# A conditioned transformer block on one core: first norms through four columns, and the last output products by a seven-product scheme

## The chip, the cores and the metric

The kernel runs on one core of one Trainium2 chip. The metric is the device time of one launch in microseconds (us). Before the change the median of three runs is 2432.27 us, with 2431.27 the lowest and 2441.08 the highest.

## What is computed

`x` is 4 x 1024 x 512 and `t` (the condition) 4 x 128, all in float32. One block with 16 heads of 32 and a hidden width of 2048 is applied, and its input is added once more at the end:

```
norm(x, t, gw, gb, bw, bb):
    g, b = t @ gw.T + gb, t @ bw.T + bb
    return g * x * rsqrt(mean(x*x) + 1e-6) + b
attention(x): q, k, v = x @ Wq.T, x @ Wk.T, x @ Wv.T
    softmax(q k.T / sqrt(32)) v, then @ Wo.T
x1  = x  + attention(norm(x, t, g1..., b1...))
x2  = x1 + (silu(h @ gate_w.T) * (h @ hid_w.T)) @ out_w.T,  h = norm(x1, t, g2..., b2...)
out = x + x2
```

## The kernel before, in words

Features lie on the 128 partitions and tokens along the free axis. The tokens are cut into 8 blocks of 512 (`NBLK`), two for each of the 4 batch items; the 512 features are 4 chunks of 128 (`C`).

**Start (L707 to L738).** The first two blocks are loaded, and `norm_sum` (L210) makes the inverse root of the first: ScalarE (ACT) squares each chunk (L215), TensorE (PE) sums it over the partitions by a product with a constant matrix `ones_mean` (L216), which leaves the mean in all 128 partitions; ACT takes the root (L218), VectorE (DVE) the reciprocal (L219), each over 128x512. `modulation` (L718) makes the gains and shifts from `t` with 8 small products. `norm_rest` scales on DVE (L199) and modulates on ACT (L202). Then keys and queries are projected (`project_kq`), the second block is normed in the same way, and values are projected (`project_v`).

**Main loop (L774, step g).** Each g computes scores for one `raw` tile (4 heads x 256 keys x 256 queries, from 10 buffers), copies them out of PSUM, takes maxima, subtracts, exponentiates, and multiplies by the values. The row sums of the softmax come from adding the exponentials of four tiles: the first tile is the accumulator, and the other three are added to it by DMAs on GpSimd's queue (L396), one after another. DVE folds the result (L404), PE sums it over partitions (`sums`, L414). There are 256 raw tiles.

From g = 60 (`FS`) on the feed-forward part of earlier blocks is worked in between, one hidden tile p of 128 in two g. Gate and hidden products are made by Winograd's form of Strassen's scheme: seven half-width products (2 matmul passes of 256 columns each) in place of eight, in the methods `pair_15` to `pair_4`; DVE and ACT make the sums between them in PSUM. The output projection is plain: four hidden tiles form a group, and each p runs one `contract` (L576) of four passes of 512 columns over the group before, for one of the 4 output chunks d. `take_contract` (L580) adds half the product to the residual `res` and, with the last group of a block, sends `out`.

**Tail (L935 to L976).** When attention is done (g = 268, p0 = 104), p runs on alone to 127, and four more `contract` calls finish group 31. `mm` (L109) splits each 128x128 weight into four 32-column parts here, which run beside each other.

**Order.** On PE, DVE, ACT and GpSimd the order is the one the program writes. SP's queue, which issues nearly all loads and stores, is ordered by the framework's scheduler, which places a DMA where it expects its buffer to be free; SP then waits in that order. The scores have four banks of PSUM (`ps_sc`), other products two (`ps`, tag `w`), one (`ps_av`) and one (`ps_b`).

Of the kernel before, what the change touches and what calls it, by code (L numbers as in the profile page):

```python
# [10 lines left out]
F32 = mybir.dt.float32  # L11
BF16 = mybir.dt.bfloat16
AF = mybir.ActivationFunctionType
ALU = mybir.AluOpType
# [3 lines left out]
P = 128  # L18
NB = 512
# [5 lines left out]
def tile_cond_transformer_block(  # L25
# [33 lines left out]
    ps_sc = ctx.enter_context(tc.tile_pool(name="ps_sc", bufs=1, space=PSUM))  # L59
    ps_av = ctx.enter_context(tc.tile_pool(name="ps_av", bufs=1, space=PSUM))  # L60
    ps = ctx.enter_context(tc.tile_pool(name="ps", bufs=2, space=PSUM))
    ps_b = ctx.enter_context(tc.tile_pool(name="ps_b", bufs=1, space=PSUM))


    ident = const.tile([P, P], F32, tag="ident", name="ident")
# [143 lines left out]

    def norm_sum(dst, tag: str):  # L210

        pm = ps.tile([P, NB], F32, tag="w", name=f"pm{tag}")
        for c in range(C):
            sq = sb.tile([P, NB], F32, tag="h", name=f"sq{tag}_{c}", bufs=7)
            nc.scalar.activation(sq, dst[:, c, :], AF.Square)  # L215
            nc.tensor.matmul(pm, ones_mean, sq, start=(c == 0), stop=(c == C - 1))  # L216
        inv = sb.tile([P, NB], F32, tag="rmax" if tag == "a0_0" else "tot", name=f"inv{tag}", bufs=1)
        nc.scalar.activation(inv, pm, AF.Sqrt, bias=eps)  # L218
        nc.vector.reciprocal(inv, inv)  # L219
# [312 lines left out]
    def pair_26(p: int):  # L532
        a = bank_a[p]
        product(a[:, LEFT], fw[p, 0][:, 1], tokens(p // NF)[2])
        product(a[:, RIGHT], fw[p, 1][:, 1], state["sums"][:, 1])
# [49 lines left out]
            nc.sync.dma_start(out=out[n][:, d, :], in_=r)  # L585


    NR = NBLK * C * (NB // HQ) * UN
    GB = C * (NB // HQ)
    BS = GB * UN  # L590
# [113 lines left out]
    with tc.manual_schedule(  # L704
# [29 lines left out]
        for kt in range(KT // 2):  # L734
            project_v(0, kt)()
            if kt == 0:
                modulation(1)
        project_kq(0, 0, 0, 1)()  # L738

# [2 lines left out]
        g = 0  # L742
        END = NR + 12
        NP_ = NBLK * NF

        def filler(p: int, tail: bool = False):
# [9 lines left out]
            if q + 1 < NP_:  # L756
# [178 lines left out]
        p0 = (END - FS) // 2  # L935
        for p in range(p0, NP_):
# [24 lines left out]
            evict()  # L961
            if p == p0:
                pm = ps.tile([P, NB], F32, tag="w", name=f"pmf{n}")
                for c in range(C):
                    nc.tensor.matmul(pm, ones_mean, squares[c], start=(c == 0), stop=(c == C - 1))
                inv = sb.tile([P, NB], F32, tag="tot", name=f"invf{n}", bufs=1)
                nc.scalar.activation(inv, pm, AF.Sqrt, bias=eps)
                nc.vector.reciprocal(inv, inv)
                state[f"f{n}"] = inv
            if p == p0 + 1:  # L970
                norm_rest(1, n // QB, x2[n], f"f{n}")
        for p in range(NP_, NP_ + FG):
            one, two, evict = filler(p)
            one()
            two()
            evict()  # L976


# [39 lines left out]
```

## Time and profile before

| what | value |
|---|---|
| median of three runs | 2432.27 us |
| profiled execution, its own time | 2435.25 us |
| its span (first to last instruction) | 2433.4 us |
| mean granted clock of TensorE | 0.998 |
| PE busy | 2378.9 us, 98% |
| DVE busy | 1938.6 us, 80% |
| ACT busy | 1412.7 us, 58% |
| accumulating DMAs (L396) | 192, 1024 KB each, 9.2 us to landing (median) |

A row of the page's groups or of the order of time gives an engine, a line of the kernel, what is written and read, and durations. PE and PEld are matmuls and the loads of their weights; a float32 product shows as two rows of each. The idle time in brackets is that of the engine before the instruction, with what released it. Ends of matmuls are modelled, and their rows overlap; the distance between starts is what counts. DMA rows on a queue (SPq, POOLq) show the issue; the time to landing stands in the table of DMA issues.

### The profile page before, as it was taken

What the parts mean: (1) busy time and instruction counts of PE and PEld (TensorE: products, weight loads), DVE (VectorE), ACT (ScalarE), POOL (GpSimd) and SP (SyncE); (2) the same over time, 40 slices, a digit from 0 to 9 for tenths busy, and PEclk for the clock granted to TensorE, in tenths of its full rate; (3) what the DMA queues carried; (4) which work ended last, traced back from release to release, by engine and by line L of the source; (5) the groups of instructions that cost most, each with busy time, mean ns of one, the idle gap of its engine ahead of it and who ended that gap; (6) DMA issues with size and microseconds to landing.
All of it is one profiled execution on the core that took longest, in us unless ns stands there. A gap on an engine that the chain in (4) does not pass through costs nothing. (4 is left out here: it accounts for less than half of the span.)

```text
span 2433.4 us, 72676 instructions
## 1 busy us (share of the span) xinstructions
PE 2378.9 (98%) x32553; PEld 1131.6 (47%) x32553; DVE 1938.6 (80%) x2183; ACT 1412.7 (58%) x1495; POOL 172.4 (7%) x207
## 2 busy tenths in 40 slices
PE   8999999999999999999999999999999999999999
PEld 3333334345454544545454545454545454434444
DVE  2688988888799988998899979997999799833322
ACT  3677777766566656755576657665666576512110
POOL 0000000000000000000000000000000000000000
PEclk9999999999999999999999999999999999999999
DMA  6599999988889788989888888898888889853442
GB/s 216 167 302 262 263 247 248 224 223 228 199 203 218 193 229 204 215 210 231 196 210 217 223 200 211 208 232 211 200 206 214 218 202 216 198 143 118 144 129 71
DMA packets 185988, 501.79 MB, mean 206 GB/s; under 512 B 21319, under 2 KB 78663, under 8 KB 158286
## 3 DMA queue, kind: packets, MB, share of 16 engines
q0 software_dynamic: 28656, 208.68, 44.3%
q1 hardware_dynamic: 156734, 288.47, 35.4%
q8 instruction: 256, 4.19, 0.7%
q14 instruction: 54, 0.44, 0.1%
q10 hardware_dynamic: 288, 0.01, 0.0%
HBM read 246.44 MB, written 41.97 MB: 119 GB/s over the span
## 5 line engine op out<-in xcount | busy, mean ns | idle before, releaser
L369 DVE TENSOR_TENSOR raw<-raw,shift 128x2048 f32<-128x2048 f32 (+1 forms) x320 | 588.8, 1856 | 26.1 <-ACT shift L364 26.1
L323 ACT COPY raw<-sc 128x2048 f32<-128x2048 f32 x256 | 479.6, 1873 | 181.6 <-PE sc L316 123.0
L372 ACT ACTIVATE raw<-raw 128x2048 f32<-128x2048 f32 x256 | 491.0, 1918 | 149.8 <-DVE raw L369 147.3
L328 DVE TENSOR_TENSOR rmax<-rmax,raw 128x1024 f32<-128x1024 f32 x384 | 469.5, 1223 | 47.5 <-ACT raw L323 41.2
L112 PE MATMUL pc<-h,ow 128*32 128x512 f32 x4096 | 469.1, 595 | 3.0 <-DMA ow<-in_out_w 2.1
L396 POOL DMA_DIRECT2D raw<-raw x192 | 165.3, 861 | 1944.9 <-ACT raw L372 864.3
L316 PE MATMUL sc<-q,k 32*128 32x256 f32 x4096 | 293.3, 400 | 1.1 <-ACT raw L323 1.1
L382 PE MATMUL av<-raw,v 128*32 128x256 f32 x4096 | 271.9, 383 | 21.6 <-ACT raw L372 21.1
L112 PE MATMUL pa<-x,fa 128*32 128x256 f32 x4096 | 269.9, 381 | 3.7 <-DVE pa L530 2.7
L112 PE MATMUL pa<-sums,fw 128*32 128x256 f32 x4096 | 267.9, 379 | 0.0
L112 PEld LDWEIGHTS pc<-h,ow 128*32 128x32 f32 x4096 | 128.3, 110 | 247.7 <-issue 226.6
L316 PEld LDWEIGHTS sc<-q,k 32*128 32x128 f32 x4096 | 184.9, 184 | 117.5 <-issue 74.9
L112 PE MATMUL pkq<-y,wkq 128*32 128x512 f32 (+1 forms) x1664 | 231.4, 594 | 4.3 <-ACT y L202 4.1
L112 PEld LDWEIGHTS pa<-x,fa 128*32 128x32 f32 x4096 | 123.4, 109 | 120.7 <-DVE pa L530 21.1
L112 PEld LDWEIGHTS pa<-sums,fw 128*32 128x32 f32 x4096 | 133.0, 110 | 88.0
L382 PEld LDWEIGHTS av<-raw,v 128*32 128x32 f32 x4096 | 110.4, 109 | 134.9 <-ACT raw L372 50.8
L583 DVE SCALAR_TENSOR_TENSOR res<-pc,res 128x512 f32<-128x512 f32 x128 | 88.2, 689 | 73.3 <-PE pc L112 70.4
L562 ACT ACTIVATE t<-pa 128x512 f32<-128x512 f32 x128 | 78.3, 611 | 109.9 <-PE pa L112 109.6
L545 ACT COPY pb<-pa 128x256 f32<-128x256 f32 x128 | 46.2, 361 | 164.3 <-PE pa L112 163.0
L112 PE MATMUL pb<-x,fw 128*32 128x256 f32 x2048 | 134.0, 379 | 1.2 <-ACT pb L545 1.2
L112 PE MATMUL pa<-x,fw 128*32 128x256 f32 x2048 | 134.0, 379 | 0.0
L112 PE MATMUL pb<-sums,fa 128*32 128x256 f32 x2048 | 133.9, 379 | 0.0
(108 smaller groups left out, 2163.9 us busy)
## 6 DMA issues: line engine op xcount, KB each, us to landing
raw<-raw POOLq DMA_DIRECT2D x192, 1024.0 KB, 9.2
fw<-sw SPq DMA_DIRECT2D x128, 512.0 KB, 7.1
fa<-in_gh_w SPq DMA_DIRECT2D x128, 384.0 KB, 6.1
ow<-in_out_w SPq DMA_DIRECT2D x128, 256.0 KB, 3.2
wkq<-in_kq_w SPq DMA_DIRECT2D x32, 512.0 KB, 6.3
v<-vs SPq DMA_DIRECT2D x128, 128.0 KB, 6.0
k<-kqs SPq DMA_DIRECT2D x124, 128.0 KB, 7.3
kqs<-st SPq DMA_DIRECT2D x61, 256.0 KB, 9.2
```

What stands on the lines that cost most here:

```text
L112: nc.tensor.matmul(dst[k : k + n, :], w[:, k : k + n], moving, start=start, stop=stop, skip_group_check=seeded)
L316: nc.tensor.matmul(sc[:, i, k, :], keys[rows, k * P : (k + 1) * P], queries[rows, :], start=True, stop=True)
L323: nc.scalar.copy(raw[r].rearrange("p k h q -> p h k q"), state.pop(("sc", r)))
L328: nc.vector.tensor_tensor(rmax[j], rmax[j], raw[r][:, k, :, :], ALU.max)
L369: nc.vector.tensor_tensor(t, t, s.unsqueeze(1).to_broadcast(list(t.shape)), ALU.add)
L372: nc.scalar.activation(raw[r], raw[r], AF.Exp)
L382: nc.tensor.matmul(av[j][i * DH : (i + 1) * DH, :], v[m, u][:, k, i * DH : (i + 1) * DH], raw[r][:, k, i, :], start=(kt == 0), stop=(kt == ...
L396: nc.gpsimd.dma_start(out=acc[j].rearrange("p k h q -> p (k h q)"), in_=raw[r].rearrange("p k h q -> p (k h q)"), accum_op=ALU.add,)
L545: nc.scalar.copy(bank_b[p][:, RIGHT], bank_a[p][:, RIGHT])
L562: nc.scalar.activation(state["t", p], bank_a[p], AF.Tanh, scale=0.5)
L583: nc.vector.scalar_tensor_tensor(r, pp, 0.5, r, ALU.mult, ALU.add)
```

## The change

It has four parts.

1. `norm_sum` for the first two blocks. The squares of the four chunks are added on DVE, and four products with a single column of `ones_mean` bring the means of the 512 tokens into 128 partitions x 4 columns. Root and reciprocal work on these four columns. DVE multiplies an identity matrix by them (`diagonal`), and one product of `ones_mean` with the diagonal spreads the inverse to all partitions, into PSUM (`spread_root`), from where the scaling reads it. The two tiles of the inverse in SBUF go.
2. `warm` multiplies constants: five products ahead of the first norm, one before and one after its spread. The second norm's spread comes after the first value projection.
3. From p = 108 (`seven`) on, and for the last group, the output projection uses the scheme of seven products over pairs of output chunks and pairs of hidden tiles (`output_steps`). Four banks are taken from the scores' pool, which is closed at p0, and two of them are seeded with a constant product. The weights of all four groups are loaded once into `raw` buffers, 16 loads of 256 KB (`output_sums`), and their sums are made on DVE at p = 106 to 109 (`output_sums_add`); the sums of the hidden halves are made on DVE at the end of each group (`hidden_sums`). Loads of `ow` stop at q = 103.
4. The last group runs both pairs of chunks in turn, step by step, in place of four `contract` calls.

```diff
-        pm = ps.tile([P, NB], F32, tag="w", name=f"pm{tag}")
+        sq = [sb.tile([P, NB], F32, tag="h", name=f"sq{tag}_{c}", bufs=7) for c in range(C)]
         for c in range(C):
-            sq = sb.tile([P, NB], F32, tag="h", name=f"sq{tag}_{c}", bufs=7)
-            nc.scalar.activation(sq, dst[:, c, :], AF.Square)
-            nc.tensor.matmul(pm, ones_mean, sq, start=(c == 0), stop=(c == C - 1))
-        inv = sb.tile([P, NB], F32, tag="rmax" if tag == "a0_0" else "tot", name=f"inv{tag}", bufs=1)
-        nc.scalar.activation(inv, pm, AF.Sqrt, bias=eps)
-        nc.vector.reciprocal(inv, inv)
-        state[tag] = inv
+            nc.scalar.activation(sq[c], dst[:, c, :], AF.Square)
+            if c:
+                nc.vector.tensor_tensor(sq[0], sq[0], sq[c], ALU.add)
+        nt = NB // P
+        pm = ps.tile([P, nt], F32, tag="w", name=f"pm{tag}")
+        for t in range(nt):
+            nc.tensor.matmul(pm[:, t : t + 1], sq[0][:, t * P : (t + 1) * P], ones_mean[:, 0:1], start=True, stop=True)
+        few = sb.tile([P, nt], F32, tag="few", name=f"few{tag}", bufs=2)
+        nc.scalar.activation(few, pm, AF.Sqrt, bias=eps)
+        nc.vector.reciprocal(few, few)
+        diagonal = sb.tile([P, nt, P], F32, tag="t", name=f"diagonal{tag}", bufs=2)
+        nc.vector.scalar_tensor_tensor(
+            diagonal, ident..., float(D), few..., ALU.mult, ALU.mult)
+
+        def spread_root():
+            inv = ps.tile([P, NB], F32, tag="w", name=f"inv{tag}")
+            nc.tensor.matmul(inv, ones_mean, diagonal.rearrange("p t q -> p (t q)"), start=True, stop=True)
+            state[tag] = inv
+        return spread_root
...
+    def output_sums(f: int, k: int):
+        w = sb.tile([P, 16, P], F32, tag="raw", name=f"wt{f}_{k}", bufs=RAW)
+        for i in range(2):
+            nc.sync.dma_start(out=w[:, 4 * i : 4 * i + 4, :], in_=out_w[f, 2 * k + i])
+        state["wt", f, k] = w
+
+    def output_sums_add(f: int, k: int):
+        w = state["wt", f, k]
+        a11, a12, a21, a22, s1, s2, s3, s4 = (w[:, i : i + 2, :] for i in range(0, 16, 2))
+        nc.vector.tensor_tensor(s1, a21, a22, ALU.add)
+        nc.vector.tensor_tensor(s2, s1, a11, ALU.subtract)
+        nc.vector.tensor_tensor(s3, a11, a21, ALU.subtract)
+        nc.vector.tensor_tensor(s4, a12, s2, ALU.subtract)
+
+    def hidden_sums(gr: int):
+        t = sb.tile([P, 4, 2, HQ], F32, tag="raw", name=f"ht{gr}", bufs=RAW)
+        one, two = hidden_halves(gr, 0), hidden_halves(gr, 1)
+        for i in range(4):
+            for k in range(2):
+                b11, b12, b21, b22 = one[k][:, LEFT], one[k][:, RIGHT], two[k][:, LEFT], two[k][:, RIGHT]
+                a, b = ((b12, b11), (b22, t[:, 0, k]), (b22, b12), (b21, t[:, 1, k]))[i]
+                nc.vector.tensor_tensor(t[:, i, k], a, b, ALU.subtract)
+        state["ht", gr] = t
+
+    def output_steps(gr: int, k: int):
...
+        def step_1():
+            times(a[:, 0], a11, left(one), True)
+        def step_5():
+            times(a[:, 1], s1, sums_of(0))
+            p5.append(sb.tile([P, HQ], F32, tag="avs", name=f"o5_{gr}_{k}", bufs=2))
+            nc.scalar.copy(p5[0], a[:, 1])
+            nc.vector.tensor_tensor(a[:, 1], a[:, 0], p5[0], ALU.add)
+        def step_26():
+            times(a[:, 0], a12, left(two))
+            times(a[:, 1], s2, sums_of(1))
+            nc.scalar.copy(b[:, 1], a[:, 1])
+        def step_7():
+            times(b[:, 1], s3, sums_of(2))
+            nc.vector.tensor_tensor(b[:, 0], b[:, 1], p5[0], ALU.subtract)
+        def step_3():
+            times(a[:, 1], s4, right(two))
+            take(0, a)
+        def step_4():
+            times(b[:, 0], a22, sums_of(3))
+            take(1, b)
...
-        norm_sum(y[0, 0], "a0_0")
+        warm(5)
+        spread_root = norm_sum(y[0, 0], "a0_0")
...
         modulation(0)
+        warm(1)
+        spread_root()
+        warm(1)
         norm_rest(0, 0, y[0, 0], "a0_0")
         evicts = [project_kq(0, 0, which, 0) for which in range(2)]
-        norm_sum(y[0, 1], "a0_1")
+        spread_root = norm_sum(y[0, 1], "a0_1")
         for evict in evicts:
             evict()
+        project_v(0, 0)()
+        spread_root()
         norm_rest(0, 0, y[0, 1], "a0_1")
...
+        scores_pool.__exit__(None, None, None)
+        ps_out = ctx.enter_context(tc.tile_pool(name="ps_out", bufs=1, space=PSUM))
+        state["outs"] = [ps_out.tile([P, 2, HQ], F32, tag=f"o{i}", name=f"outs{i}") for i in range(4)]
...
+            if i % 2 == 0:
+                return (lambda: (one(), five())), two_six, (lambda: None)
+            return (lambda: (seventh(), three())), four, (lambda: None)
         for p in range(p0, NP_):
...
+            if p < p0 + NF // FG:
+                for k in range(2):
+                    output_sums((seven // FG - 1 + p - p0) % (NF // FG), k)
...
-            one, two, evict = filler(p, True)
+            one, two, evict = filler(p, True) if p < seven else last_filler(p)
...
+            if p0 + 1 < p <= p0 + 1 + NF // FG:
+                for k in range(2):
+                    output_sums_add((seven // FG - 1 + p - p0 - 2) % (NF // FG), k)
+            if p % FG == FG - 1 and p >= seven - 1:
+                hidden_sums(p // FG)
-        for p in range(NP_, NP_ + FG):
-            one, two, evict = filler(p)
-            one()
-            two()
-            evict()
+        one, other = (output_steps(NP_ // FG - 1, k) for k in range(2))
+        one[0]()
+        other[0]()
+        for i in range(1, 6):
+            one[i]()
+            other[i]()
```

More of the change, by code (lines that the diff above doesn't have):

```diff
@@ L58, in tile_cond_transformer_block @@
     sb = ctx.enter_context(tc.tile_pool(name="sb", bufs=1))
-    ps_sc = ctx.enter_context(tc.tile_pool(name="ps_sc", bufs=1, space=PSUM))
     ps_av = ctx.enter_context(tc.tile_pool(name="ps_av", bufs=1, space=PSUM))
@@ L62, in tile_cond_transformer_block @@
     ps_b = ctx.enter_context(tc.tile_pool(name="ps_b", bufs=1, space=PSUM))
+    scores_pool = tc.tile_pool(name="ps_sc", bufs=1, space=PSUM)
+    ps_sc = scores_pool.__enter__()
     ident = const.tile([P, P], F32, tag="ident", name="ident")
@@ L210, in norm_sum @@
     def norm_sum(dst, tag: str):
-        pm = ps.tile([P, NB], F32, tag="w", name=f"pm{tag}")
+        sq = [sb.tile([P, NB], F32, tag="h", name=f"sq{tag}_{c}", bufs=7) for c in range(C)]
         for c in range(C):
-            sq = sb.tile([P, NB], F32, tag="h", name=f"sq{tag}_{c}", bufs=7)
-            nc.scalar.activation(sq, dst[:, c, :], AF.Square)
-            nc.tensor.matmul(pm, ones_mean, sq, start=(c == 0), stop=(c == C - 1))
-        inv = sb.tile([P, NB], F32, tag="rmax" if tag == "a0_0" else "tot", name=f"inv{tag}", bufs=1)
-        nc.scalar.activation(inv, pm, AF.Sqrt, bias=eps)
-        nc.vector.reciprocal(inv, inv)
-        state[tag] = inv
+            nc.scalar.activation(sq[c], dst[:, c, :], AF.Square)
[10 more added lines that the diff above has]
+        nc.vector.scalar_tensor_tensor(
+            diagonal,
+            ident.unsqueeze(1).to_broadcast([P, nt, P]),
+            float(D),
+            few.unsqueeze(2).to_broadcast([P, nt, P]),
+            ALU.mult,
+            ALU.mult,
+        )
+        def spread_root():
[3 more added lines that the diff above has]
+        return spread_root
     def norm_rest(which: int, b: int, dst, tag: str):
@@ new lines, in hidden_halves @@
+    def hidden_halves(gr: int, i: int):
+        return [h[gr * FG + 2 * i + k] for k in range(2)]
+    def hidden_sums(gr: int):
[7 more added lines that the diff above has]
+        state["ht", gr] = t
@@ new lines, in output_steps, with times, left, right @@
+    def output_steps(gr: int, k: int):
+        banks = state["outs"]
+        a, b = banks[2 * k], banks[2 * k + 1]
+        w = state["wt", gr % (NF // FG), k]
+        a11, a12, _, a22, s1, s2, s3, s4 = (w[:, i : i + 2, :] for i in range(0, 16, 2))
+        one, two, t = hidden_halves(gr, 0), hidden_halves(gr, 1), state["ht", gr]
+        p5 = []
+        def times(dst, weights, moving, start: bool = False):
+            for i in range(2):
+                mm(dst, weights[:, i, :], moving[i], start and i == 0, i == 1, True)
+        def left(tiles):
+            return [x[:, LEFT] for x in tiles]
+        def right(tiles):
+            return [x[:, RIGHT] for x in tiles]
+        def sums_of(i):
+            return [t[:, i, 0], t[:, i, 1]]
+        def take(d: int, bank):
+            n, d = gr * FG // NF, 2 * k + d
+            r = res[n][:, d, :]
+            nc.vector.scalar_tensor_tensor(r, bank.rearrange("p a q -> p (a q)"), 0.5, r, ALU.mult, ALU.add)
+            if gr % (NF // FG) == NF // FG - 1:
+                nc.sync.dma_start(out=out[n][:, d, :], in_=r)
+        def step_1():
[18 more added lines that the diff above has]
+            take(1, b)
+        return step_1, step_5, step_26, step_7, step_3, step_4
@@ L715, in tile_cond_transformer_block, with warm @@
         fetch()
-        norm_sum(y[0, 0], "a0_0")
+        def warm(count: int):
+            ahead = ps.tile([P, NB // P, P], F32, tag="w", name="ahead")
+            for _ in range(count):
+                nc.tensor.matmul(
+                    ahead, ones_mean, ones_mean.unsqueeze(1).to_broadcast(list(ahead.shape)), start=True, stop=True
+                )
+        warm(5)
+        spread_root = norm_sum(y[0, 0], "a0_0")
         def modulation(k: int):
@@ L727, in tile_cond_transformer_block @@
         modulation(0)
+        warm(1)
+        spread_root()
+        warm(1)
         norm_rest(0, 0, y[0, 0], "a0_0")
         evicts = [project_kq(0, 0, which, 0) for which in range(2)]
-        norm_sum(y[0, 1], "a0_1")
+        spread_root = norm_sum(y[0, 1], "a0_1")
         for evict in evicts:
             evict()
+        project_v(0, 0)()
+        spread_root()
         norm_rest(0, 0, y[0, 1], "a0_1")
-        for kt in range(KT // 2):
+        for kt in range(1, KT // 2):
             project_v(0, kt)()
-            if kt == 0:
+            if kt == 1:
                 modulation(1)
@@ L744, in tile_cond_transformer_block @@
         NP_ = NBLK * NF
+        seven = ((END - FS) // 2 // FG + 1) * FG
         def filler(p: int, tail: bool = False):
@@ L755, in filler @@
                 pp = ps.tile([P, NB], F32, tag="w", name=f"pc{q}")
-            if q + 1 < NP_:
+            if q + 1 < seven - FG:
                 load_ow(q + 1)
@@ L935, in tile_cond_transformer_block, with last_filler @@
         p0 = (END - FS) // 2
+        scores_pool.__exit__(None, None, None)
+        ps_out = ctx.enter_context(tc.tile_pool(name="ps_out", bufs=1, space=PSUM))
+        state["outs"] = [ps_out.tile([P, 2, HQ], F32, tag=f"o{i}", name=f"outs{i}") for i in range(4)]
+        for i in (1, 3):
+            nc.tensor.matmul(
+                state["outs"][i].rearrange("p a q -> p (a q)"),
+                select[:, 0, :],
+                select.rearrange("p h c -> p (h c)"),
+                start=True,
+                stop=True,
+            )
+        steps = {}
+        def last_filler(p: int):
+            gr, i = (p - FG) // FG, p % FG
+            if i % 2 == 0:
+                steps[gr, i // 2] = output_steps(gr, i // 2)
+            one, five, two_six, seventh, three, four = steps[gr, i // 2]
+            if i % 2 == 0:
+                return (lambda: (one(), five())), two_six, (lambda: None)
+            return (lambda: (seventh(), three())), four, (lambda: None)
         for p in range(p0, NP_):
```

## The prediction

> **What bounds the kernel now.** I read the page first, then the order of time of the first 60 us, of the end of the attention and of the last 60 us, then the waits of the matrix engine.
>
> ```profile
> PE 2378.9 (98%) x32553; PEld 1131.6 (47%) x32553; DVE 1938.6 (80%) x2183; ACT 1412.7 (58%) x1495; POOL 172.4 (7%) x207
> ...
> PE   8999999999999999999999999999999999999999
> ...
> DVE  2688988888799988998899979997999799833322
> ```
>
> TensorE (PE) is busy from end to end, and its waits come to under 50 us, so a microsecond counts only if it is taken from PE's row. It can be gained in the first slice (8 tenths), by giving PE less to do, or lost by making it wait.
>
> ```profile
> 7.07 0.63 ACT L215 ACTIVATE sqa<-y 128x512 f32<-128x512 f32 x1 [0.34 <-DMA y<-in_x]
> ...
> 11.58 0.69 ACT L218 ACTIVATE inva<-pma,eps 128x512 f32<-128x512 f32 x1 [2.58 <-PE pma L216]
> ...
> 12.30 3.35 DVE L219 RECIPROCAL inva<-inva 128x512 f32<-128x512 f32 x1 [9.94 <-ACT inva L218]
> ...
> 15.69 2.50 DVE L199 TENSOR_TENSOR y<-y,inva 128x512 f32<-128x512 f32 x4
> 16.41 2.93 ACT L202 ACTIVATE y<-y,mod 128x512 f32<-128x512 f32 x4 [4.15 <-DVE y L199]
> ...
> 17.28 8.88 PE L112 MATMUL pkq<-y,wkq 128*128 128x512 f32 x16 [4.06 <-ACT y L202]
> ...
> 26.00 3.60 PE L216 MATMUL pma<-sqa,ones_mean 128*128 128x512 f32 x8
> ...
> 30.37 3.70 PE L112 MATMUL pv<-wv,y 128*128 128x512 f32 x8 [0.78 <-ACT inva L218]
> ...
> 33.91 1.84 PE L722 MATMUL pmod<-condT,modw 128*128 128x4 f32 x16
> ...
> 50.33 1.15 PE L316 MATMUL sc<-q,k 32*128 32x256 f32 x16
> ```
>
> Columns: start, duration, engine and line, operands, idle before. The last square is done at 7.70, yet the first real product starts at 17.28, since a norm of 512 columns is summed, rooted and inverted (3.35 us) in full width. Each of the 16 rows of pkq should take 0.43 us (the weight loads are 0.43 us apart from 20.85 on), 6.9 us in all; it takes 8.88 because the first come 0.85 us apart. Scores begin at 50.33.
>
> ```profile
> 2117.51 0.86 POOL L396 DMA_DIRECT2D raw<-raw  x1 [11.37 <-ACT raw L372]
> ...
> 2126.96 0.86 POOL L396 DMA_DIRECT2D raw<-raw  x1 [8.59 <-DMA raw<-raw]
> ...
> 2139.51 0.86 POOL L396 DMA_DIRECT2D raw<-raw  x1 [11.70 <-DMA raw<-raw]
> ...
> 2148.89 1.22 DVE L404 TENSOR_TENSOR raw<-raw 128x1024 f32<-128x1024 f32 x1 [3.06 <-DMA raw<-raw]
> ...
> 2150.22 0.64 PE L414 MATMUL sum<-raw,ones_sum 128*32 128x256 f32 x8 [3.06 <-DVE raw L404]
> ```
>
> Here a DMA sets PE's pace: the last three accumulating DMAs (raw blocks 253, 254, 255) go one after another, each waiting for the one before, and PE stands 3.06 us until the third has landed and been folded. There is no slack in this chain.
>
> ```profile
> 2397.68 1.05 PE L112 MATMUL pa<-x,fa 128*32 128x256 f32 x16
> ...
> 2407.16 1.05 PE L112 MATMUL pa<-x,fa 128*32 128x256 f32 x16
> ...
> 2413.19 15.63 PE L112 MATMUL pc<-h,ow 128*32 128x512 f32 x144
> ...
> 2428.89 0.69 DVE L583 SCALAR_TENSOR_TENSOR res<-pc,res 128x512 f32<-128x512 f32 x1 [2.74 <-PE pc L112]
> ```
>
> The tail runs with no gap: 9.48 us from p to p+1 for 22 half-width units (14 of the gate and hidden products, 8 of the output), so 0.431 us a unit.
>
> **Part 1, the start.** After the last square (7.70) a third add on DVE, 0.69 as the 128x512 rows of L199, ends at 8.45. Four products with one column: the row is pmod, 8 products in 1.84, so 0.92 and a drain, to 9.65. Root and inverse of 4 columns have no row; reciprocals take 3.35 for 512 and 1.75 for 256 columns, so some 0.15 fixed; I take 0.2 and 0.1 (ends: 0.06, the 128x1 memset, and 0.69, the full root). A 0.41 us copy stands between on DVE, then the diagonal, 0.69 like L583: 11.15. PE meanwhile does modulation (1.84, to 11.5), one constant product (0.86) and, at 12.35, the spread (0.86, to 13.2). Scaling 0.69, modulation 0.80: PE starts at 14.85 and not 17.28. Warm, pkq takes 6.9 and ends at 21.7 (26.0 before). The second norm costs PE 0.92 and not 3.60, and its bank comes free after a tiny root: pv starts at 23.05 (30.37 before). Then pv 3.43, spread 0.86, pv 3.43, modulation 1.84 and three chains of 3.43: scores at 42.9. Gain 7.4 us. The second norm's scaling (27.5 to 31.2) hides under pv. Reading the inverse from PSUM costs nothing: the L570 row, with a PSUM operand, is 0.69 as well. Loads don't stop it: modw and wkq, issued at 2.61 and 3.08, land 6.0 and 6.6 us later.
>
> The constant products rest on the clock. The Trainium skill (TensorE: Matmul & The Clock Gate, "The HAM clock gate") says that the array runs at half rate until it was busy for a window of about 3.4 us, and falls back after an idle one. The rows: busy from 5.16, weight loads 0.85 apart until 10.44; again from 17.28 to 20.85. By the rule at its best the five (ten passes) from 1.05 end at 7.1, by the first row (5.3 us cold) at 7.9: both before 8.45, so the sum is the same. If the clock fell back, pkq would pay 1.7 to 2.0 again.
>
> **Part 2, seven products.** Groups 26 to 31 get 28 half-width units in place of 32. Inside the loop 5 groups x 4 x 0.431 = 8.6 us less. The last group alone saves 1.7, and loses it: its sums (8 subtractions of 128x256, 0.42 each by L480) queue on DVE behind hidden and take, so the first waits about 0.1, and its a12 product waits for an add standing behind all eight: 1.6. Net 0. At p = 108 DVE holds the take (to 0.94 after PE's start of the step), eight weight sums (3.35) and the first token difference (0.42), 4.7, and PE, after 1.72 + 0.86, is there at 2.6: a stall of 2.2. At p = 112, 116, 120, 124 the difference is ready at 1.4 to 2.0: none. Two seeding products in bf16: 0.45. ACT gets one 0.36 copy per p, DVE 0.4 to 3.4; both have over half of the 9.48 free. Removed loads of ow are hidden today. The last four outs now leave within 2.6 us and not 10.6: 256 KB each, 2.5 us to landing; I take 0.2 (0 to 1). Sum: 8.6 - 2.2 - 0.45 - 0.2 = 5.8 us gained.
>
> **Part 3, the moved loads.** In the built order, 16 loads of 256 KB for the output weights stand on SP's queue not in the tail but from about 2091 on, where the scheduler finds raw buffers coming free. Several wait for an accumulating DMA: wt2_1 for block 249, wt3_1 for 250, wt0_0 for 251, wt0_1 for 253, wt1_1 for 254. Behind them in the queue are fw100 to fw103, fa100 to fa103 and ow98. Those have cover: fw101, behind wt0_0, would be issued near 2118 instead of 2107, needs 8 to 9 us and is used at 2133.3; fw103 near 2142, used at 2158. The accumulates have none. Of the 192 in the trace, 146 had less than 0.8 MB of SP's traffic in their first 7.5 us, and landed after 9.0 us on average; 25 had 1.1 to 1.8 MB, and took 11.5. The Trainium skill (Trainium Kernel Development and Optimization, "Key Constraints") says that the queues of SP, ACT and POOL run on the same 16 DMA engines and interleave; it speaks against the change. By separate paths this part would cost 0; by the shared ones, with wt0_0, fw101, fa101 and fw102 beside block 253, this takes 11.5 and not 8.9 (+2.6); block 254 is already slow (12.0 beside the 1 MB of res), say -0.5; block 255 gets wt1_1 and all that was held behind it, 11.5 to 12 and not 9.4 (+2.4). PE stands 4.5 us longer. It comes back cold as it does today (pc at 2151.34 takes 5.01 and not 3.6); half a microsecond more. I take 5.0 (ends: 0, and 12.6 when all three take 14.3, the longest seen).
>
> **Sum.** 7.4 + 5.8 - 5.0 = 8.2 us. On the profiled execution (2435.25, span 2433.4) that gives 2427.1; it lies 3.0 above the median, so 2432.27 - 8.2 = 2424.
>
> **Rivals.**
> - The loads are covered: part 3 costs at most 1, all else as above: 2419 to 2420. For it: DMA engines are at 5 tenths in the slice after 2129. Against: PE's 3.06 us wait sits there already.
> - The start gives half: the clock falls back between the tiny products, or part of the earlier scores is lost in waiting for exponentials (21 us of PE's waits are av on ACT): 7.4 becomes 3.5, 2428; with a stall more in the tail 2431.
> - Slower: the wait that SP's queue stands in. If blocks 250 and 251 also take 14.3, 251 lands 1.5 late for its fold, fw101 is issued at 2126 and comes 3 late, and the last three cost 12.6: 17 lost against 13.2 gained, 2436. It decides from 13.2 us of added standing on; cold restarts in each gap would add 2 to 4.
>
> **Chances.** The likeliest case (2420.5 to 2429) 0.50; loads covered 0.30; half a start 0.12; slower 0.08. About 0.5%, 12.2 us, is what a measurement of this kernel can tell from no change. Faster by more (under 2420.1): the second case and the edge of the first, 0.34; within: 0.60; slower by more (over 2444.4): the worst of the last, 0.06. The range 2415 to 2435 leaves out the far part of the last case and the edge of the second.[...]
>
> **What would show it.** Right: scores start near 43; in the tail four p take 36.2 and not 37.9; one stall near 2 us at p = 108; the wait of the last sum on the fold grows from 3 to about 8, with accumulates of 11 to 12 us. Wrong: scores after 46, a wait of PE on fw, fa or wt, or a fold wait that stays at 3.

## The result and the profile after

The changed kernel takes 2425.51 us (median of six runs, 2422.81 to 2427.8); the kernel before, six runs beside it, 2435.43 (2431.27 to 2441.08). The ratio is 0.9958 with a 95% interval of 0.9948 to 0.9968: about 10 us faster. The span of the profiled execution went from 2433.4 to 2424.1 us, 9.3 less; the forecast was 8.2 less, from 2432.27 to 2424. The time lies within the likeliest case, but none of the terms came out as put: the start brought less, the moved loads cost less and the tail brought more, and the clock took a loss that no term had. That the sum fits is in part luck.

The busy line and two rows of the page of the changed kernel:

```profile
PE 2374.3 (98%) x33149; PEld 1153.2 (48%) x33149; DVE 1975.1 (81%) x2295; ACT 1420.1 (59%) x1519; POOL 172.4 (7%) x207
...
PE   9999999999999999999999999999999999989999
...
DVE  2688888889799988998899979997999799835544
```

PE's first digit is now 9 and a new 8 has come in slice 36, which covers 2121 to 2182 us: there stands the longer wait on the last fold. DVE's last three slices go from 3, 2, 2 to 5, 4, 4: the sums of the seven products, still far from a bound. PE's busy time fell by only 4.6 us, although products of over 8 us were taken out: the rows of the seven constant products alone add 8.9 us (6.10, 1.68 and 1.13).

**The start**, in order of time (start, duration, engine and line, operands, idle before):

```profile
7.93 1.05 PE L222 MATMUL pma<-ones_mean,sqa 128*128 128x1 f32 x8 [0.77 <-DVE pick L83]
8.84 1.93 PE L839 MATMUL pmod<-condT,modw 128*128 128x4 f32 x16
9.02 0.26 ACT L224 ACTIVATE fewa<-pma,eps 128x4 f32<-128x4 f32 x1 [0.88 <-PE pma L222]
9.31 0.18 DVE L225 RECIPROCAL fewa<-fewa 128x4 f32<-128x4 f32 x1 [1.38 <-ACT fewa L224]
9.72 0.67 DVE L227 SCALAR_TENSOR_TENSOR diagonala<-ident,fewa 128x512 f32<-128x512 f32 x1
10.63 1.68 PE L828 MATMUL ahead<-ones_mean 128*128 128x512 f32 x2
12.36 2.07 PE L238 MATMUL inva<-diagonala,ones_mean 128*128 128x512 f32 x2
...
14.47 2.48 DVE L200 TENSOR_TENSOR y<-y,inva 128x512 f32<-128x512 f32 x4 [3.48 <-PE inva L238]
...
16.07 7.13 PE L113 MATMUL pkq<-y,wkq 128*128 128x512 f32 x16 [0.70 <-ACT y L203]
...
24.34 3.70 PE L113 MATMUL pv<-wv,y 128*128 128x512 f32 x8 [0.35 <-ACT fewa L224]
...
44.49 1.15 PE L337 MATMUL sc<-q,k 32*128 32x256 f32 x16
```

Root, reciprocal and diagonal cost what was forecast. What is new is the pair of rows at 10.63 and 12.36: a product of 512 columns takes two passes, about 0.43 apart, so that its row is 1.02 to 1.12 long; here the rows are 1.68 and 2.07. The clock was down (granted 0.86 and 0.65; the stretches stand in the first experiment). Scores begin at 44.49 and not at 50.33 (5.84 gained), nor at the forecast 42.9.

**The last accumulating DMAs:**

```profile
2112.89 0.86 POOL L417 DMA_DIRECT2D raw<-raw  x1 [10.52 <-ACT raw L393]
...
2123.55 0.86 POOL L417 DMA_DIRECT2D raw<-raw  x1 [9.80 <-DMA raw<-raw]
...
2135.24 0.86 POOL L417 DMA_DIRECT2D raw<-raw  x1 [10.83 <-DMA raw<-raw]
...
2146.20 1.23 DVE L425 TENSOR_TENSOR raw<-raw 128x1024 f32<-128x1024 f32 x1 [4.98 <-DMA raw<-raw]
...
2147.53 0.90 PE L435 MATMUL sum<-raw,ones_sum 128*32 128x256 f32 x8 [4.98 <-DVE raw L425]
```

From the issue of block 253 to the fold it is 33.31 us (31.38 before), and PE's wait grew from 3.06 to 4.98, not to 8.

**Where the 9.3 us went**, by the lead that the changed kernel has over the one before at the same product: 5.84 at the first scores; 4.15 at 140 us (the clock fell back once more, below); 4.61 at 2120 (most of the difference at 588 us, where PE waited 1.53 us and not 2.08); 2.69 after the last fold; 2.05 at p0; 0.3 behind the stall at p = 108; then 0.83 more for every two p; 9.27 at the last product's take.

### The profile page after: what moved, and what is told of

It is laid out like the page before. It is cut to its first block, busy times and chain, and to the rows that moved or that the text cites. A ratio compares the mean times of both kernels' runs of the same rounds, so it can differ in the third digit from the quotient of the medians.

```text
span 2424.1 us, 74021 instructions
## 1 busy us (share of the span) xinstructions
PE 2374.3 (98%) x33149; PEld 1153.2 (48%) x33149; DVE 1975.1 (81%) x2295; ACT 1420.1 (59%) x1519; POOL 172.4 (7%) x207
## 5 line engine op out<-in xcount | busy, mean ns | idle before, releaser
L113 PE MATMUL pc<-h,ow 128*32 128x512 f32 x3328 | 379.9, 595 | 2.5 <-ACT raw L393 1.5
L113 PEld LDWEIGHTS pc<-h,ow 128*32 128x32 f32 x3328 | 103.7, 110 | 206.9 <-issue 193.0
L113 PEld LDWEIGHTS pkq<-y,wkq 128*32 128x32 f32 (+1 forms) x1664 | 72.6, 117 | 125.3 <-issue 117.4
L385 ACT COPY shift<-sp 128x512 f32<-128x512 f32 x128 | 75.0, 586 | 95.0 <-PE sp L113 95.0
```

The costliest lines, as they stand in the source:

```text
L113: nc.tensor.matmul(dst[k : k + n, :], w[:, k : k + n], moving, start=start, stop=stop, skip_group_check=seeded)
L385: nc.scalar.copy(shift[j][:, k : k + 2, :], pp)
```

## The experiments

All kernels were run beside the kernel before. "Scores" is the start of the first scores in the trace, "chain" the time from the issue of block 253 to the last fold, with the time of the last block alone in brackets, "wait" PE's wait on that fold. These columns are of one trace each, which need not be the median execution.

| kernel | median us | ratio to before, 95% interval | span | scores | chain (last block) | wait |
|---|---|---|---|---|---|---|
| before | 2435.43 | | 2433.4 | 50.33 | 31.38 (9.38) | 3.06 |
| changed | 2425.51 | 0.9958 [0.9948, 0.9968] | 2424.1 | 44.49 | 33.31 (10.96) | 4.98 |
| start alone | 2427.97 | 0.9964 [0.9949, 0.9979] | 2428.6 | 43.21 | 31.00 (8.46) | 2.67 |
| tail alone | 2433.15 | 0.9982 [0.9973, 0.9991] | 2431.8 | 50.98 | 33.15 (11.10) | 4.82 |
| loads on ACT | 2423.31 | 0.9942 [0.9927, 0.9957] | 2421.1 | 44.97 | 28.25 (8.02) | none |
| no constant products | 2430.99 | 0.9981 [0.9972, 0.9991] | 2428.7 | 47.03 | 32.59 (10.99) | 4.26 |
| sixth product ahead | 2424.63 | 0.9958 [0.9943, 0.9973] | 2421.9 | 44.62 | 32.21 (11.21) | 3.88 |
| order on DVE | 2423.40 | 0.9949 [0.9933, 0.9966] | 2423.4 | 43.15 | 32.40 (10.96) | 4.07 |
| three edits together | 2417.80 | 0.9929 [0.9916, 0.9942] | 2415.4 | 44.72 | 29.96 (8.20) | 1.64 |
| full products between | 2424.90 | 0.9956 [0.9941, 0.9970] | 2430.3 | 49.26 | 33.47 (11.40) | 4.71 |
| the same once more | 2427.49 (one run) | | 2425.7 | 44.39 | 33.52 (11.42) | 5.19 |
| three edits, other start | 2418.72 | 0.9933 [0.9920, 0.9945] | 2413.7 | 44.79 | 28.25 (8.23) | none |

By their intervals, the tail alone and the kernel without constant products are slower than the changed kernel, and the two kernels with three edits are faster. The other single edits are not told apart from it by their times; what they are worth is read from the traces.

### The two halves apart

The kernel before with only the changed `norm_sum` and the start that goes with it; the output keeps its eight products:

```diff
-        norm_sum(y[0, 0], "a0_0")
+        warm(5)
+        spread_root = norm_sum(y[0, 0], "a0_0")
...
+        warm(1)
+        spread_root()
+        warm(1)
```

> Only the start is changed (short norms and constant products); the tail, its banks and its loads are those of before. Theory (the moved weight loads lengthen the last accumulating DMAs): without them PE's wait for the last fold is back at 3.1 us and the last sum lies as much ahead of before as the scores of g = 60 to 250, 4 to 6 us; span 2428 to 2430, ratio 0.998. Rival (PE comes earlier to a chain of DMAs that has its own pace): the wait grows to about 5 here too, though no load has moved, and the span is 2430 to 2431.

Its wait on the fold is 2.67 (3.06 before), so the longer wait does not come from the earlier start. And its scores begin at 43.21, with a lead of 7.12: the forecast start, step by step. Its rows, for the same work as above:

```profile
8.17 1.05 PE L221 MATMUL pma<-ones_mean,sqa 128*128 128x1 f32 x8
9.08 1.93 PE L751 MATMUL pmod<-condT,modw 128*128 128x4 f32 x16
10.87 1.10 PE L740 MATMUL ahead<-ones_mean 128*128 128x512 f32 x2
12.03 1.12 PE L237 MATMUL inva<-diagonala,ones_mean 128*128 128x512 f32 x2
12.99 1.02 PE L740 MATMUL ahead<-ones_mean 128*128 128x512 f32 x2
14.79 7.13 PE L112 MATMUL pkq<-y,wkq 128*128 128x512 f32 x16 [0.77 <-ACT y L202]
```

PE starts on pkq at 14.79; the forecast was 14.85. Here the fifth constant product ran until the first sum could start (no idle before pma) and the clock held. The same stretches of time of the changed kernel, and then of this one (stretch, length, PE busy and rows, granted clock, DMA share, GB/s):

```profile
8.50:12.00 3.50, 3.50 (x23) 0.86 0.93 298
12.00:15.50 3.50, 3.30 (x5) 0.65 1.00 418
```

```profile
8.50:12.00 3.50, 3.47 (x25) 1.00 1.01 334
12.00:15.50 3.50, 2.70 (x6) 1.00 1.01 421
```

PE's row is full in the first pair while the clock falls, so the row alone does not show whether the clock will hold.

The other half, the changed kernel with `norm_sum` and the start of before:

```diff
-        warm(5)
-        spread_root = norm_sum(y[0, 0], "a0_0")
+        norm_sum(y[0, 0], "a0_0")
```

> Only the tail is changed (seven products, their banks, their loads); the start is that of before. Theory: the last sum comes about 2 us later than before (wait 5 in place of 3.1), the tail from there on is 6.5 to 7 us shorter, span 2428 to 2429, ratio 0.998; with the start alone the gains add up to that of the whole change. Rival (the loads cost nothing): wait 3.1, span 2426 to 2427.

The wait is 4.82 and the last block takes 11.10: the longer wait belongs to the tail's edits, as the theory had it. The span is 3 us above what was expected, for a reason outside the edit: the clock fell back twice more than in the profiled execution of before (granted 0.67 at 35 to 40 us and about 0.83 at 590 to 600), and the lead at 620 us was -2.4. From the seeding products to the last take it needs 237.96 us, the changed kernel 238.19.

By the ratios of the medians the start alone is worth 8.8 us and the tail alone 4.4, 13.2 together, and the whole change 10.2. The intervals are 2 to 4 us wide to each side, so this neither confirms nor contradicts that the two gains add up.

### The loads of the output weights

The 16 loads on ACT's queue, where they stay in the written order and so come at p = 104 to 107, behind the last accumulate:

```diff
-            nc.sync.dma_start(out=w[:, 4 * i : 4 * i + 4, :], in_=out_w[f, 2 * k + i])
+            nc.scalar.dma_start(out=w[:, 4 * i : 4 * i + 4, :], in_=out_w[f, 2 * k + i])
```

> The changed kernel, with the 16 loads of the output weights issued on ACT's queue at p = 104 to 107, where the program writes them, and so after the last accumulating DMA. Theory: blocks 253, 254 and 255 take what they took before, the wait for the last fold is near 3.1 and the span 2 us under that of the changed kernel (2422), if ACT's issues do not delay the copy before the seventh product; each issue 0.4 us, four in a p. Rival (no contention): wait stays near 5, span 2424 or more.

The wait is gone altogether: less than the 3.06 of before. With the loads among the accumulates, seven traces give 10.96 to 11.42 us for the last block; the five without them, old and new start, give 8.02 to 9.38. That is what these loads cost, together with the loads that they hold up in SP's queue, and it is shown. That the chain fell below that of before goes with something else. SP's load of `res` (1 MB) waits until a store of `out` has landed, and that took 2.8 us in this trace and 8.0 to 8.6 before and in the start alone. In this trace, then in the start alone:

```profile
2114.41 0.34 SPq L606 DMA_DIRECT2D out<-res  x1
...
2117.30 0.59 SPq L456 DMA_DIRECT2D res<-in_x  x1
```

```profile
2113.01 0.34 SPq L605 DMA_DIRECT2D out<-res  x1
...
2121.64 0.33 SPq L455 DMA_DIRECT2D res<-in_x  x1
```

So `res` was issued here 3.3 us after block 253 and ran beside it, not beside 254. From its issue to the next, 254 took 9.70 us, where it took 12.55 before and 12.06 in the start alone. Why the store landed sooner isn't shown.

Not all of it reached the end. At p = 105 ACT's copy now came late behind its own DMA issues, and the clock fell behind that wait. First this wait in the changed kernel, then in this one:

```profile
2209.54 1.07 PE L113 MATMUL pb<-x,fw 128*32 128x256 f32 x16 [1.20 <-ACT pb L566]
```

```profile
2205.11 1.25 PE L113 MATMUL pb<-x,fw 128*32 128x256 f32 x16 [2.05 <-ACT pb L566]
...
2206.11 1.95 PE L113 MATMUL pa<-x,fw 128*32 128x256 f32 x16
```

16 products of `pa` took 1.95 where 1.05 is usual. The queue that loads are moved to needs room too.

### The constant products

```diff
-        warm(5)
...
-        warm(1)
...
-        warm(1)
```

> The changed kernel without its seven constant products. Theory: the short norms bring most of the start's gain, the products only the clock. PE then starts on pkq somewhat earlier (near 14, since neither constant product stands before it), runs it at half clock for one window, and the scores start 1 to 2 us later than in the changed kernel (45.5 to 46.5). Rival (the products are what makes the start faster): scores after 48. Second rival (the products stand in the way): scores before 44.5.

Scores at 47.03, between the two expectations: 2.5 us later than in the changed kernel and 3.8 later than in the start alone. Without these products the one-column sums took 1.87 (1.05 warm), the modulation 3.55 (1.93), the spread 2.05, and pkq 8.56. So in the start they are worth about 4 us where the clock holds, and 2.5 where it falls back as in the changed kernel's trace. The medians lie further apart, by some 5.6 us, and this trace loses another 1.5 us on the changed kernel's between 140 and 2120 us; why isn't shown. (The granted clock of that trace reads 1.00 in those stretches; the length of the rows tells more than that column there.)

The idle time of 0.77 us between the fifth constant product and the first sum looked like the reason for the fall. A sixth closes it:

```diff
-        warm(5)
+        warm(6)
```

> The changed kernel with six constant products ahead and not five. Theory: in the changed kernel PE stands idle for 0.77 us between the fifth constant product and the first one-column sum (1.15 us in the run with the loads on ACT), and the clock falls back for some 7 us after it (granted 0.86 and 0.65); in the run with the new start alone, where the constant products ended only with the squares, there was no gap, the clock stayed at 1.00, and scores began at 43.21. A sixth product of 0.86 us closes the gap: granted clock 1.00 from 8.5 us to the scores, scores at 43.2 to 43.7 in place of 44.49, the time 0.8 to 1.3 us below that of the changed kernel. Rival: the one-column and four-column products are too little work for the clock in any case; it falls to 0.6 to 0.8 again somewhere between 8.5 and 19 us, and scores begin at 44.5 or later.

The theory fell: there was no idle time, and the clock fell all the same, later. The spread took 1.74 and the constant product behind it 1.91; scores at 44.62. The next attempt put full-width products among the small ones, in case the small ones hardly count for the clock. All constant products also write to another bank of PSUM here (the pool `ps_av`):

```diff
-            ahead = ps.tile([P, NB // P, P], F32, tag="w", name="ahead")
+            ahead = ps_av.tile([P, NB // P, P], F32, tag="av", name="ahead")
...
             for i in range(k * 2 * C, (k + 1) * 2 * C):
+                if k == 0 and i == C:
+                    warm(1)
                 nc.tensor.matmul(pm[:, i, :], modw[:, i * P : (i + 1) * P], condT, start=True, stop=True)
...
+        warm(1)
         modulation(0)
```

> The changed kernel (five constant products ahead) with two full-width constant products more: one between the one-column sums and the first modulation, one in the middle of that modulation. Theory, formed after the sixth product ahead did not help: what counts for the clock is how much of some 3.4 us full-width products fill, and one-column and four-column products hardly count. The starts so far fit it: the clock held where three full-width products fell close together (scores at 43.21 and 43.15) and fell back some 6.5 us after it had risen where only one or two did (44.49, 44.97, 44.62, 44.72). With the two products there is one of 0.86 us in every 1.8 us: granted clock 1.00 from 8.5 us on, the products before pkq never above 1.15 for two passes, the spread 0.5 later than at best, scores at 43.5 to 43.9. Rival: half-filled stretches aren't enough or it is something else; clock below 0.9 in one of the stretches from 8.5 to 19 us, scores at 45 or later.

> The same kernel once more, for its start alone, since the clock held in one run of a kernel and fell in another: the theory has it at 1.00 from 8.5 us to the scores in every run (scores at 43.5 to 43.9); by the rival it falls in this run or in the one before.

The two executions of this one kernel disagree. In the first:

```profile
1.06 6.03 PE L828 MATMUL ahead<-ones_mean 128*128 128x512 f32 x10 [1.06 <-DVE eps L75]
8.70 1.05 PE L222 MATMUL pma<-ones_mean,sqa 128*128 128x1 f32 x8 [1.61 <-DVE pick L83]
...
11.81 2.05 PE L828 MATMUL ahead<-ones_mean 128*128 128x512 f32 x2
...
49.26 0.93 PE L337 MATMUL sc<-q,k 32*128 32x256 f32 x12
```

and in the second:

```profile
1.06 7.17 PE L828 MATMUL ahead<-ones_mean 128*128 128x512 f32 x10 [1.06 <-DVE eps L75]
8.06 0.95 PE L222 MATMUL pma<-ones_mean,sqa 128*128 128x1 f32 x8
...
11.56 0.95 PE L841 MATMUL pmod<-condT,modw 128*128 128x4 f32 x8
...
44.39 1.15 PE L337 MATMUL sc<-q,k 32*128 32x256 f32 x16
```

The five constant products took 6.03 us in one and 7.17 in the other, that is, the clock came up earlier or later. Over all nine traces with constant products: where five ended early (6.03 to 6.14) and idle time of 0.77 to 1.61 followed, the clock fell, three times of three; where five ended late (7.14 to 7.50), with no idle time, it held, four times of four; with six (7.91 and 8.01), also without idle time, it fell, twice of two. So neither idle time nor small products explain it alone (the start alone held with the same small products), and two more full products cost 1.2 us on the path where the clock would have held without them (44.39 against 43.15 and 43.21).

What decides can be read from the clock records of the twelve traces. The granted clock changes only on a grid: each whole stretch at half clock is 3.41, 6.83 or 10.24 us long, and those at full clock are whole multiples of 3.41. Where the grid lies differs from one execution to the next; with constant products the clock first rises at 4.06 to 7.00 us. The traces have 8461 grid stretches at full clock, and 39 of them end in a fall (12 of these at the end of the program). As an estimate of how far a stretch is filled, count 0.43 us for each float32 pass of 512 columns (as the rows show), other widths in proportion and bf16 half of it; a product with one column then counts next to nothing. The 39 are filled to at most 0.395, all the others to at least 0.40, but for one at the very end of a trace (0.37).

In the changed kernel the stretch from 7.62 to 11.03 us holds part of the idle time and the small products and is filled to 0.135. Where five constant products ended late, the grid divides the small products between two stretches, each filled to 0.49 or more. With six, the sixth product falls into the stretch before, and the next, with the small ones, comes to 0.37 and 0.39. In the first run with full products between, most of the 1.61 us of idle time falls into the stretch from 7.47 us (0.26). So the theory of that run was right about what counts, but the place of the grid is not the program's to choose.

### DVE's order in the tail

The differences of the hidden tokens ahead of the sums of weights at p = 107, and in the last group only half of them ahead of the adds of the fifth step (the argument `which` is new):

```diff
...
-            if p0 + 1 < p <= p0 + 1 + NF // FG:
-                for k in range(2):
-                    output_sums_add((seven // FG - 1 + p - p0 - 2) % (NF // FG), k)
             if p % FG == FG - 1 and p >= seven - 1:
-                hidden_sums(p // FG)
+                hidden_sums(p // FG, range(2 if p == NP_ - 1 else 4))
+            if p0 + 1 < p <= p0 + 1 + NF // FG:
+                for k in range(2):
+                    output_sums_add((seven // FG - 1 + p - p0 - 2) % (NF // FG), k)
...
             other[i]()
+            if i == 1:
+                hidden_sums(NP_ // FG - 1, range(2, 4))
```

> The changed kernel with another order on DVE in the tail: at p = 107 the eight differences of the hidden tokens stand ahead of the eight sums of weights, and in the last group the third and fourth pair of differences stand behind the two adds of the fifth step. Theory: the stall of 1.5 us at p = 108 and that of 0.73 us in the last group are DVE's order alone; both go below 0.3, and the stretch from the last seeding product to the end is 1.8 to 2.2 us shorter. Rival: the eight sums (3.35 us) now stand ahead of the adds that the next gate product waits for, and PE loses 0.8 to 1.5 us there: the tail gains at most 1 us.

The stall in the changed kernel, and what is left of it here:

```profile
2229.33 1.07 PE L113 MATMUL outs<-ht,wt 128*32 128x256 f32 x16 [1.49 <-DVE ht L635]
```

```profile
2233.62 1.07 PE L113 MATMUL pb<-sums,fa 128*32 128x256 f32 x16 [0.19 <-DVE pb L573]
```

Both stalls are gone, a new one of 0.19 has come, and from the seeding products to the last take it is 236.25 us and not 238.19: 1.94 less, from two changes of order.

### Together

The order on DVE, a sixth constant product, and the loads on ACT with two to a p from p = 106 on:

```diff
-            if p < p0 + NF // FG:
-                for k in range(2):
-                    output_sums((seven // FG - 1 + p - p0) % (NF // FG), k)
+            if p == p0:
+                for k in range(2):
+                    output_sums((seven // FG - 1) % (NF // FG), k)
+            elif p0 + 2 <= p < p0 + 2 * NF // FG:
+                output_sums((seven // FG - 1 + (p - p0) // 2) % (NF // FG), (p - p0) % 2)
...
-            if p0 + 1 < p <= p0 + 1 + NF // FG:
+            if p - p0 in (2, 5, 9, 13):
...
```

> The changed kernel with six constant products ahead, the order on DVE of the run before, and the loads of the output weights issued on ACT at p = 104 and, two to a p, from p = 106 to 111 (the run with all loads on ACT had 16 at p = 104 to 107, and there ACT's copy came 2.05 us late at p = 105). Theory: the three terms add: start 0.8 to 1.3, order 2, loads 5 (the wait on the fold and the clock's fall behind it gone, without the 2.05 us wait at p = 105): span 2415 to 2417, 7 to 9 us below the changed kernel. Rival: that the wait on the fold was gone in the run with loads on ACT was the luck of the load of res, issued at 2117.3 there and at 2121.6 in the run with the new start alone, where the last three accumulates took 31.0 us and not 28.3; then a wait of 2.5 to 3 us on the fold comes back, with a slow clock behind it, and the span is 2418.5 to 2421.

2417.80 us, a ratio of 0.9929 with an interval of 0.9916 to 0.9942, which lies wholly below that of the changed kernel: both kernels are beaten. The wait at p = 105 is back at 1.20. `res` was issued 1.98 us ahead of block 254 here (1.50 in the start alone, 0.99 before), 254 took 10.91 (12.06, 12.55), and a wait of 1.64 was left; the clock did not fall behind it. The start gained nothing, as in the run with the sixth product alone. So the span of 2415.4 is within what was expected, but not by its terms: no gain in the start, and instead 1.5 us more lead at 2120 us, since the clock did not fall at 134 us as in the changed kernel (below).

The same with five constant products ahead and the two full products between in place of the sixth, written to `ps_av` as in that run:

```diff
...
-        warm(6)
+        warm(5)
...
+                if k == 0 and i == C:
+                    warm(1)
...
+        warm(1)
         modulation(0)
```

> The combined kernel (order on DVE in the tail, loads of the output weights on ACT spread over p = 104 to 111) with this start in place of the sixth product ahead. Theory: scores at 43.5 to 43.9 in place of 44.72, and so a span of 2414.3 or less and a median about 1 us below 2417.8, if the wait on the last fold stays at 0 to 2 us. Rival: the clock falls in the start again, scores at 45 or later and no gain.

The start was not better (44.79), though the clock held; the median, 2418.72, does not tell the two kernels apart. Its trace shows the end of the attention with no wait at all:

```profile
2131.53 0.86 POOL L417 DMA_DIRECT2D raw<-raw  x1 [8.68 <-DMA raw<-raw]
...
2139.76 1.22 DVE L425 TENSOR_TENSOR raw<-raw 128x1024 f32<-128x1024 f32 x1
...
2141.07 0.64 PE L435 MATMUL sum<-raw,ones_sum 128*32 128x256 f32 x8
2142.20 3.64 PE L113 MATMUL pc<-h,ow 128*32 128x512 f32 x32 [0.48 <-ACT total L440]
```

`res` was issued at 2114.8 this time, again 3.3 us after block 253, and 254 took 9.54, as in the first run on ACT. `pc` takes 3.64 where it took 4.75 after the wait of 4.98.

## Why the prediction was right, and where its steps were off

The total was right: 8.2 forecast, 9.3 in the span, 0.9958 in the medians. The mechanisms were right in the main; the sizes of the terms were not. Point by point:

- **The start, 7.4 forecast, 5.84 measured.** The steps were right: with the clock up it is 7.12 and 7.18, in the two traces with this start in which the clock held there (the start alone, and the order on DVE). The missing 1.3 is a term that the prediction had named but not put into the sum: the clock fell between the small products. The prediction said that pkq would pay 1.7 to 2.0 again in that case; in fact the constant product and the spread paid, and pkq ran warm (7.13, forecast 6.9).
- **A loss that no step had, 1.7.** At 132 to 138 us the clock fell once more. In order of time in the changed kernel:

```profile
131.28 1.15 PE L337 MATMUL sc<-q,k 32*128 32x256 f32 x16 [0.80 <-ACT raw L344]
...
133.56 1.66 PE L403 MATMUL av<-raw,v 128*32 128x256 f32 x16 [1.13 <-ACT raw L393]
```

The same two waits in the kernel before, where the clock held:

```profile
137.40 1.15 PE L316 MATMUL sc<-q,k 32*128 32x256 f32 x16 [1.07 <-ACT raw L323]
...
139.41 1.07 PE L382 MATMUL av<-raw,v 128*32 128x256 f32 x16 [0.86 <-ACT raw L372]
```

The two waits come to 1.93 us in both kernels, and to 1.93 or 1.94 in all twelve traces. What differs is how they lie on the grid of the clock. Two grid stretches of the changed kernel, and then of the second run with full products between, whose scores began 0.1 us earlier (stretch, length, PE busy, granted clock, DMA share, GB/s):

```profile
130.50:133.91 3.41, 1.50 (x24) 1.00 1.06 246
133.91:137.32 3.41, 3.41 (x28) 0.50 1.01 276
```

```profile
129.22:132.63 3.41, 2.21 (x24) 1.00 1.05 291
132.63:136.05 3.42, 2.58 (x32) 1.00 1.01 219
```

In the first, nearly all of the two waits lies in one stretch, and the next runs at half clock; in the second the grid divides them. The clock fell here in five of the ten traces with the new start (the stretch filled to 0.31 to 0.40, by the estimate above) and held in the other five and in both with the old one (none under 0.48). So whether this loss comes is chance from one execution to the next. It is about as large as the error of the start, and the trace of before, where the grid divides the waits, did not show it.
- **The tail, 5.8 forecast, 6.6 measured** from the last fold to the end (2.69 to 9.27). Four p take 36.26 us and not 37.91, 1.65 a group for 1.72 forecast (8.25 and not 8.6 over five). The stall at p = 108 was 1.49, not 2.2; with the restart behind it the lead fell by 1.7. The prediction counted DVE's take, eight sums and a difference one behind another; in the trace one sum starts 0.33 to 0.46 after the last, less on average than its 0.42 of length, so the eight need 2.9 and not 3.35: 0.4 of the 0.7 too much. The seeds cost 0.54 (0.45). The last group was to bring nothing and brought about 0.7: its stall was 0.73 and not 1.6. The four outs together cost nothing (0.2).
- **The moved loads, 5.0 forecast, 1.9 measured.** The mechanism was right, and the price of the last block too: 2.4 forecast, 10.96 for 9.38 in the pair of traces, and on average 11.15 (seven traces) for 8.92 (before and start alone). The term that failed is that of block 253, +2.6: the loads issued beside it moved only 0.09 MB in its first 7.5 us (0.54 before), and it landed after 10.1 us, in the start alone, without these loads, after 10.0. The 8.9 from which the prediction counted is the lowest of the five traces without these loads (8.9 to 10.3); the seven with them have 8.2 to 11.6, so the loads' price on this block isn't shown. And 254, put at -0.5, became 0.9 shorter. Beside the last block SP's queue moved 1.6 MB in the first 7.5 us, within the 1.1 to 1.8 MB of the accumulates from which the prediction took its 11.5, and it landed after 10.9. That TensorE would restart slower was counted at 0.5 and cost nothing: the slow restart is the same as before (`pc` 4.75, 5.01 before).
- **The rule that was set against the change** (the Trainium skill, "Trainium Kernel Development and Optimization", "Key Constraints": the queues of SP, ACT and POOL share the 16 DMA engines) holds here: 11.0 to 11.4 us with company, 8.0 to 9.4 without.
- **The rivals.** The start's half gain did not come as put, though 1.6 of it did. "Loads covered" is false: the run with the loads on ACT shows what they cost. The slow case, SP's queue standing so long that fw comes late, did not come: no wait of PE on fw, fa or wt is in the trace.

So the errors were -1.6 (start), -1.7 (clock at 134 us), +3.1 (loads), +0.8 (tail) and +0.5 in between: +1.1 together. A sum that fits hides four terms that don't, and that they cancel was luck.

## What to carry to other kernels

When loads are added to a program whose queue is ordered by a scheduler, look up where they land in the built order, and not where they were written; among transfers on which the bound engine waits they cost (1.9 us of PE's time here), and a queue that keeps the written order puts them behind. A row of small products keeps PE's row full but need not keep its clock: read the length of a known full-width product beside the granted clock, and don't count on a clock that two executions of one kernel grant differently: what held it here was wide products in over 0.4 of each 3.41 us, wherever these began. In a step that feeds the bound engine, what others wait for goes first on the helping engine: two changes of order on DVE were worth 1.9 us, and both stalls stood in the changed kernel's trace.

## What the runs showed of the hardware

- The clock falls with much less idle time than the rule has on which the constant products rest. The Trainium skill ("TensorE: Matmul & The Clock Gate", "The HAM clock gate") has half rate after an idle window of about 3.4 us. The traces agree with the length: the granted clock changes on a grid of 3.41 us. But the stretch need not be idle. It fell after all those that moving columns filled to less than 0.40 by the estimate above, one at the end of a trace aside, and after none that was fuller: so after waits of 0.80 and 1.13 us within 3.1 us, after 2.05 us at p = 105, and with less than 0.1 us of idle time at a stretch in the start with six constant products. It held after 1.57 us at 153 us and after 1.64 us on the fold. The length of one wait does not decide: near 590 us the same products wait for a load or for ACT in all twelve traces, and the clock held after 2.08, 2.12, 2.40 and 2.63 us, which the grid divides, and fell after 2.20, 2.24, 2.25 and 2.34. The longest wait, in the start alone, and one of the others, in the second run with full products between (the same 32 products take 3.64 us and 5.32):

```profile
587.47 3.64 PE L112 MATMUL pc<-h,ow 128*32 128x512 f32 x32 [2.63 <-DMA ow<-in_out_w]
```

```profile
586.59 5.32 PE L113 MATMUL pc<-h,ow 128*32 128x512 f32 x32 [2.25 <-DMA ow<-in_out_w]
```

The page's remark that the window runs free of the program fits the grid, whose place changed with the execution, so that the same kernel held its clock in one and lost it in another.
- A store of 256 KB issued 0.4 us behind an accumulate of 1 MB landed after 2.8 or 2.9 us in two traces and after 8.0 to 8.6 in others, with the same instructions around it; what waits for it in SP's queue moves with it, here 1 MB of `res` from one accumulate to the next.
- An accumulate of 1 MB beside which SP's queue moved 1.6 to 1.7 MB in the first 7.5 us took 11.0 to 11.4 us to its fold (the last block in the seven traces with the moved loads there), and 8.0 to 9.4 us beside 0.2 to 0.5 MB (the five others).
